# One PSUM bank, two kinds of turn: reads by VectorE in one quarter, writes by TensorE in the next

## The chip, the cores and the metric

The kernel runs on one core of one Trainium2 chip. The metric is the device time of the whole kernel in microseconds, here the median of three runs. The core has five engines with a queue of instructions each: TensorE (PE in the profile, its weight loads PEld), VectorE (DVE), ScalarE (ACT), GpSimd (POOL) and SyncE (SP), and 16 DMA engines. Each engine takes its instructions in the order in which they were written; semaphores make an instruction wait for one on another engine.

## The reference

The input is 16 images of 64 channels and 128 x 128 pixels, in f32. Four layers follow each other, each with a group normalisation ahead of it and a residual sum around it:

```python
x = x + L0(_gn(x))   # gram = xf xf^T / N;  y = gram xf;  out = conv_w y   (all 64 x 64 per image)
x = x + L1(_gn(x))   # |Scharr x| + |Scharr y| of each channel
x = x + L2(_gn(x))   # shift of some channels by a column, 3x3 convolution, bias
x = x + L3(_gn(x))   # 3x3 convolution, 1x1 convolution, batch norm over all images, leaky ReLU, clip
```

`_gn(v)` divides channels into 32 groups of two, subtracts the mean of a group in one image and divides by its standard deviation. So each image needs, between two layers, a few numbers per channel that come from sums over the image. The batch norm of the last layer needs sums over all images.

## The kernel before

Channels lie on 64 of the 128 partitions; the other 64 hold the other half of the image (or the other parity of its rows). An image is worked in eight chunks of eight rows (`NS` = 8, `R` = 8).

The main loop runs over steps (`step`), and each step over four quarters (`q` = 0 to 3). In one step, up to four stages work on different images: `Layer3` on image b from step 8b + 35, `Layer2` from 8b + 25, `Front` (layer 0 and the Scharr filter of layer 1) from 8b + 15, and `Gram`, which turns image rows into columns and builds the 64 x 64 product of an image that the front needs later. From image 7 on `Gram` takes eight steps for an image, for images 1 to 6 four. So the first some 20 steps are a ramp, in which stages come in one by one, and then eight steps repeat for each image. When all images are through, the last pass reads two arrays back, applies the batch norm and writes the output.

Nothing is scheduled: `InOrder` (line 63) keeps every engine's instructions in the order in which the Python code names them, and all of them show line 73 in the profile. Where an instruction stands in its engine's queue is thus set by step, quarter, and place within the quarter.

The small operations that turn sums into coefficients are written as generators, here called chains. After the work of a quarter, `tick()` (line 257) lets each live chain run to its next `yield`. There are two kinds.

- `coefficients` (line 280) makes the group norm's scale and shift from 16 partial sums: a reduction to `s2` on DVE, a product with a constant matrix on PE that averages over the group, then `rstd`, which computes a square root on ACT and one correction on DVE. It is started in quarter 0, by `Front` in step 8b + 23 and by `Layer2` in step 8b + 33.
- `gram_chain` (line 304) computes, from the Gram matrix of image b, the 128 x 128 weights `abd` of layer 0 and the coefficients of the next group norm. It has seven links of a product on PE and small DVE work on its result: with `gs` (to `gd`), `st`, `dd`, `rc`, `ad` (with `vv`), `pp`, and `st1`; after the second and the last product `rstd` follows with a root on ACT. For images 2 to 6 it starts at the end of a step, in quarter 3; from image 7 it starts in quarter 2 of step 8b - 9, and the `while` in it holds it until step 8b - 4.

All products of all chains go to one bank of PSUM, `bank` (lines 178 to 185): `sm(n)` hands out columns of it. From image 7 the Gram product itself also accumulates there. A read by DVE in the bank and a write by PE in it are ordered by semaphores even where they touch different columns, so a product waits for all reads that are written ahead of it, and a read for all products ahead of it.

Names that recur below: `one` and `two` are the PSUM tiles of a 3 x 3 convolution, `c` is the copy of `one` that ACT makes (lines 896 and 954), `d` the differences of rows that DVE makes for it, `qd` its shifted copies (by a DMA from POOL's queue in layer 2, by ACT in layer 3), `xh` the normalised rows for the Scharr filter, `u` and `e` its working tiles on DVE, of which ACT takes the absolute values, `xw` the columns for the Gram product, `sd` the result of a root, `nv` its operand, `junk` the output of a square whose sum is kept.

Of the kernel before, what the change touches and what calls it, by code (L numbers as in the profile page):

```python
# [21 lines left out]
NS = HH // R  # L22
EARLY = 3
# [85 lines left out]
def tile_kernel(ctx: ExitStack, tc: tile.TileContext, x, cw_h, w2_t, b2, wbin_t, w1_t, b1, gamma, beta, consts, out):  # L109
# [10 lines left out]
    def k(name):  # L120
        return kc[:, AT[name][0]:AT[name][1]]
# [41 lines left out]
    def sv(name, n=1):  # L163
        return small.tile([P, n], F32, tag=name, name=name)
# [6 lines left out]
    def small_product(dst, wt, src):  # L171

        for o in (1 - last[0], last[0]):
            pe.matmul(dst[cols(o)], wt[:, cols(o)], src, start=True, stop=True)
        last[0] = o
# [5 lines left out]
    def sm(n, rows=P):  # L181
        if n > 8:
            return bank[0:rows, P:P + n]
        turn[0] = (turn[0] + 1) % 16
        return bank[0:rows, 8 * turn[0]:8 * turn[0] + n]
# [67 lines left out]

    now = [0]
    chains = []

    def tick():
        for c in list(chains):
            if next(c, chains) is chains:
                chains.remove(c)  # L260

    def rstd(mE, r, me, eps=None):

        dve.tensor_copy(me, mE)
        nv = sv("nv")
        dve.scalar_tensor_tensor(nv, me[:, 0:1], me[:, 0:1], me[:, 1:2], op0=ALU.mult, op1=ALU.subtract)
        if eps is not None:
            dve.tensor_scalar_sub(nv, nv, eps)
        sd = sv("sd")
        act.activation(sd, nv, AF.Sqrt, scale=-1.0)  # L270
        yield
        r0 = sv("r0")
        dve.reciprocal(r0, sd)

        e = sv("e")
        dve.scalar_tensor_tensor(e, nv, r0, r0, op0=ALU.mult, op1=ALU.mult)
        dve.tensor_scalar(e, e, 0.5, 1.5, op0=ALU.mult, op1=ALU.add)
        dve.tensor_mul(r, r0, e)

    def coefficients(st, put, back=None):  # L280

        s2 = sv("s2", 2)
        dve.tensor_reduce(s2, st, axis=AX.X, op=ALU.add)
        yield
        pm = sm(2)
        small_product(pm, k("gmean"), s2)
        yield
        co = sv("co", 2) if back is None else sv("co2", 6)
        me = sv("me", 2)
        r, mean = co[:, 0:1], me[:, 0:1]  # L290
        yield from rstd(pm, r, me, GN_EPS)
        dve.scalar_tensor_tensor(co[:, 1:2], mean, -1.0, r, op0=ALU.mult, op1=ALU.mult)
        if back is not None:

            dve.reciprocal(co[:, 2:3], r)
            dve.tensor_mul(co[:, 3:4], co[:, 2:3], k("left"))
            dve.tensor_mul(co[:, 4:5], co[:, 2:3], k("right"))
            dve.tensor_add(co[:, 5:6], mean, back)
        put(co)
# [4 lines left out]
    def gram_chain(b, pg):  # L304

        gs = stp.tile([P, C + 1], F32, tag="gs", name=f"gs_{b}", bufs=2)
        if b > 2 * EARLY:
            dve.tensor_reduce(gs, pg.rearrange("p (j c) -> p c j", j=3), axis=AX.X, op=ALU.add)
        else:
            dve.tensor_copy(gs, pg)  # L310
        if b > 1:
            yield
        while b > 2 * EARLY and now[0] < NS * b - 4:
            yield
        gd = sm(C + 1)
        small_product(gd, k("same"), gs)
        yield
        g = stp.tile([P, C + 1], F32, tag="g", name=f"g_{b}", bufs=1)
        dve.tensor_scalar_mul(g, gd, 1.0 / HW)
        mu = g[:, C:C + 1]  # L320
        st = sv("st0", 2)
        dve.tensor_copy(st[:, 0:1], mu)

        junk0 = stp.tile([P, C], F32, tag="junk0", name=f"junk0_{b}", bufs=1)
        dve.scalar_tensor_tensor(
            junk0, g[:, 0:C], GN_EPS, k("Id"), op0=ALU.add, op1=ALU.mult, accum_out=st[:, 1:2]
        )
        if b > 1:
            yield
        pm = sm(2)  # L330
        small_product(pm, k("gavg"), st)
        yield
        r, me = sv("r"), sv("me", 2)
        yield from rstd(pm, r, me)

        vv = sv("vv", 3)
        dve.tensor_copy(vv[:, 0:1], mu)
        dve.tensor_sub(vv[:, 1:2], mu, me[:, 0:1])
        dve.tensor_scalar_mul(vv[:, 2:3], me[:, 0:1], -1.0)
        dd = stp.tile([P, 2, C], F32, tag="dd", name=f"dd_{b}", bufs=1)  # L340
        for s in range(2):
            dve.tensor_scalar_mul(dd[:, s, :], k("Id"), vv[:, s:s + 1])
        if b > 1:
            yield

        pr = sm(2 * C)
        small_product(pr, k("all"), dd.rearrange("p s c -> p (s c)"))
        yield

        t0 = stp.tile([P, C], F32, tag="t0", name=f"t0_{b}", bufs=1)  # L350
        dve.scalar_tensor_tensor(t0, pr[:, 0:C], vv[:, 0:1], g[:, 0:C], op0=ALU.mult, op1=ALU.subtract)
        cs = stp.tile([P, 2, C], F32, tag="cs", name=f"cs_{b}", bufs=1)
        for s in range(2):
            dve.scalar_tensor_tensor(cs[:, s, :], pr[:, C:2 * C], vv[:, 1:2], t0, op0=ALU.mult, op1=ALU.subtract)
        rc = stp.tile([P, C], F32, tag="rc", name=f"rc_{b}", bufs=1)
        dve.tensor_scalar(rc, cwh, r, 0.5, op0=ALU.mult, op1=ALU.mult)
        csf = cs.rearrange("p s c -> p (s c)")
        if b > 1:
            yield
        pq = sm(C)  # L360
        small_product(pq, csf, rc)
        yield
        r2 = sv("r2")
        dve.tensor_mul(r2, r, r)
        for s in range(2):
            rows = slice(s * C, (s + 1) * C)
            dve.tensor_scalar_mul(wbd[rows, rows], pq[rows], r2[rows])
        ad = stp.tile([P, C], F32, tag="ad", name=f"ad_{b}", bufs=1)
        dve.scalar_tensor_tensor(ad, pq, r2, k("Id"), op0=ALU.mult, op1=ALU.add)
        abd = stp.tile([P, P], F32, tag="abd", name=f"abd_{b}", bufs=EARLY + 3)  # L370
        dve.tensor_add(abd, wbd, k("I"))
        if b > 1:
            yield
        pd = sm(C + 3)
        small_product(pd[:, 0:C], csf, ad)
        small_product(pd[:, C:C + 2], abd, vv[:, 0:2])
        small_product(pd[:, C + 2:C + 3], wbd, vv[:, 2:3])
        yield
        pp = stp.tile([P, 2, C], F32, tag="pp", name=f"pp_{b}", bufs=1)
        dve.tensor_mul(  # L380
            pp, pd[:, 0:C].unsqueeze(1).to_broadcast([P, 2, C]), ad.unsqueeze(1).to_broadcast([P, 2, C])
        )
        av = sv("av", 3)
        dve.tensor_copy(av, pd[:, C:C + 3])
        if b > 1:
            yield
        pk = sm(1)
        small_product(pk, pp.rearrange("p s c -> p (s c)"), k("q"))
        if b > 1:
            yield  # L390
        bias = av[:, 2:3]
        st1 = sv("st1", 2)
        dve.tensor_add(st1[:, 0:1], av[:, 0:1], bias)
        t = sv("t1")
        dve.scalar_tensor_tensor(t, av[:, 1:2], av[:, 1:2], pk, op0=ALU.mult, op1=ALU.subtract)
        dve.scalar_tensor_tensor(
            st1[:, 1:2], st1[:, 0:1], st1[:, 0:1], t, op0=ALU.mult, op1=ALU.subtract
        )
        if b > 1:
            yield  # L400
        pm = sm(2)
        small_product(pm, k("gavg"), st1)
        yield

        co = stp.tile([P, 5], F32, tag="co1", name=f"co1_{b}", bufs=EARLY + 3)
        r, mean = co[:, 0:1], co[:, 3:4]
        yield from rstd(pm, r, co[:, 3:5], GN_EPS)
        dve.scalar_tensor_tensor(co[:, 1:2], bias, mean, r, op0=ALU.subtract, op1=ALU.mult)
        dve.reciprocal(co[:, 2:3], r)
        lead[b] = abd, co  # L410
# [18 lines left out]
    def first_gram():  # L429
# [30 lines left out]
        for link, _ in enumerate(gram_chain(0, pg)):  # L460
            if link in (2, 3, 4, 5, 6):
                rows_to_columns(1, link - 2, rows[link - 2])

    class Gram:
# [5 lines left out]
        def at(self, i, q):  # L470
            b = self.b
            n = 4 * (i - NS) + q

            self.part({1: 44, 5: 42, 9: 42}.get(n, 0))
            if n == 10:
                chains.append(gram_chain(b, self.pg))

            if i == 2 and q == 0:
                for m in range(3):
                    self.load(m)  # L480
            m = {11: 0, 13: 1, 15: 2, 19: 3, 21: 4, 23: 5, 27: 6, 31: 7}.get(4 * i + q)
            if m is not None:
                rows_to_columns(b, m, self.xr.pop(m))
                if m + 3 < NS:
                    self.load(m + 3)
# [603 lines left out]
    while chains:  # L1089
        tick()  # L1090
# [80 lines left out]
```

## Time and profile before

| | us |
|---|---|
| median of three runs | 2755.46 (2754.84 to 2756.58) |
| the profiled execution | 2756.86 |
| its span, first to last instruction | 2755.1 |
| PE busy | 2159.6 (78%) |
| DVE busy | 2192.4 (80%) |
| ACT busy | 2113.5 (77%) |
| POOL busy | 943.2 (34%) |
| mean granted TensorE clock | 0.896 |

Busy time is the sum of an engine's instructions, without waits. A share of the span is an average over stretches that have different limits, so the table alone doesn't say what bounds the kernel. Times in the views of the profile count from the start of the span. A wait is given as the engine and tile that waited, an arrow, and the engine and tile that ended last before the wait was over; a wait for several semaphores is put down to the last of them.

### The profile page before, as it was taken

What the parts mean: (1) busy time and instruction counts of PE and PEld (TensorE: products, weight loads), DVE (VectorE), ACT (ScalarE), POOL (GpSimd) and SP (SyncE); (2) the same over time, 40 slices, a digit from 0 to 9 for tenths busy, and PEclk for the clock granted to TensorE, in tenths of its full rate; (3) what the DMA queues carried; (4) which work ended last, traced back from release to release, by engine and by line L of the source; (5) the groups of instructions that cost most, each with busy time, mean ns of one, the idle gap of its engine ahead of it and who ended that gap; (6) DMA issues with size and microseconds to landing.
All of it is one profiled execution on the core that took longest, in us unless ns stands there. A gap on an engine that the chain in (4) does not pass through costs nothing. (4 is left out here: it accounts for less than half of the span.)

```text
span 2755.1 us, 46091 instructions
## 1 busy us (share of the span) xinstructions
PE 2159.6 (78%) x14804; PEld 886.9 (32%) x14804; DVE 2192.4 (80%) x3623; ACT 2113.5 (77%) x3177; POOL 943.2 (34%) x1350
## 2 busy tenths in 40 slices
PE   6578799999999999999999999999999994000000
PEld 4233333434343434343434343333334641000000
DVE  4998899899999999999999999999996335333332
ACT  4766779998989898989898989899997667333332
POOL 2055444444444444444434444454544300000000
PEclk8689899999999999999999999999999997555555
DMA  8799779898888898888888887888887768999999
GB/s 206 200 229 233 196 183 249 214 244 220 235 224 233 215 240 224 234 227 224 230 228 226 223 203 192 208 207 206 216 207 192 219 191 297 419 420 420 420 420 384
DMA packets 693601, 685.96 MB, mean 249 GB/s; under 512 B 60096, under 2 KB 580448, under 8 KB 693360
## 3 DMA queue, kind: packets, MB, share of 16 engines
q1 hardware_dynamic: 668208, 613.83, 76.0%
q0 software_dynamic: 25152, 69.18, 9.9%
q8 instruction: 119, 1.95, 0.3%
q14 instruction: 122, 1.00, 0.1%
HBM read 346.23 MB, written 268.44 MB: 223 GB/s over the span
## 5 line engine op out<-in xcount | busy, mean ns | idle before, releaser
L73 PE MATMUL two<-d,w 128*64 128x508 f32 (+2 forms) x2560 | 837.5, 587 | 0.0
L73 PE MATMUL two<-d,wi 128*64 128x508 f32 (+3 forms) x1536 | 572.7, 578 | 0.0
L73 POOL DMA_DIRECT2D qd<-d x512 | 270.8, 531 | 851.5 <-issue 295.8
L73 PE MATMUL two<-qd,pk 128*64 128x512 f32 (+1 forms) x1024 | 518.3, 587 | 10.1 <-DMA qd<-d 8.8
L73 POOL TENSOR_SCALAR edges<-v,co 64x8 f32<-64x8 f32 x512 | 397.7, 777 | 287.4 <-ACT v L73 204.0
L73 DVE TENSOR_TENSOR d<-v 128x512 f32<-128x512 f32 (+1 forms) x512 | 346.5, 679 | 58.4 <-issue 29.7
L73 PE MATMUL one<-v,w 128*64 128x508 f32 (+2 forms) x1600 | 364.6, 580 | 30.1 <-ACT c L73 30.1
L73 PEld LDWEIGHTS two<-d,w 128*64 128x64 f32 x2560 | 265.8, 136 | 326.3 <-issue 289.8
L73 PE MATMUL one<-v,wi 128*64 128x508 f32 (+3 forms) x1536 | 360.6, 602 | 1.5 <-issue 1.4
L73 ACT COPY qd<-d 64x512 f32<-64x512 f32 x512 | 315.5, 616 | 18.6 <-DVE d L73 12.5
L73 DVE SCALAR_TENSOR_TENSOR e<-e 128x1032 f32<-128x1032 f32 (+1 forms) x256 | 313.2, 1223 | 0.0
L73 ACT ACTIVATE xh<-po,co 128x128 f32<-128x128 f32 (+1 forms) x480 | 274.9, 621 | 31.0 <-PE po L73 24.9
L73 POOL TENSOR_SCALAR v<-v,kc 128x9 f32<-128x9 f32 x256 | 246.7, 976 | 11.9
L73 ACT ACTIVATE u<-u 128x1024 f32<-128x1024 f32 x128 | 135.7, 1060 | 144.2 <-DVE u L73 144.2
L73 PEld LDWEIGHTS two<-d,wi 128*64 128x64 f32 x1536 | 177.5, 136 | 193.5 <-issue 179.2
L73 ACT ACTIVATE v<-x,co 128x512 f32<-128x512 f32 (+2 forms) x368 | 235.0, 705 | 0.0
L73 DVE SCALAR_TENSOR_TENSOR y<-two,c 128x1024 f32<-128x1024 f32 x128 | 156.0, 1219 | 94.0 <-ACT v L73 68.2
L73 PE MATMUL po<-x,abd 64*64 64x512 f32 (+1 forms) x1024 | 177.7, 641 | 43.9 <-ACT xh L73 41.6
L73 PEld LDWEIGHTS one<-v,w 128*64 128x64 f32 x1600 | 124.6, 136 | 227.9 <-issue 139.5
L73 PEld LDWEIGHTS two<-qd,pk 128*64 128x64 f32 x1024 | 136.0, 136 | 151.1 <-issue 101.9
L73 DVE SCALAR_TENSOR_TENSOR u<-xh 128x1170 f32<-128x1170 f32 x128 | 175.4, 1371 | 4.8 <-ACT xh L73 4.5
L73 PEld LDWEIGHTS one<-v,wi 128*64 128x64 f32 x1536 | 109.3, 139 | 195.9 <-issue 188.3
(165 smaller groups left out, 3321.0 us busy)
## 6 DMA issues: line engine op xcount, KB each, us to landing
x<-in_x SPq DMA_DIRECT2D x256, 256.0 KB, 4.6
x_d<-u SPq DMA_DIRECT2D x512, 128.0 KB, 4.0
y_d<-y SPq DMA_DIRECT2D x512, 128.0 KB, 3.8
x_d<-x SPq DMA_DIRECT2D x496, 128.0 KB, 2.8
xr<-in_x SPq DMA_DIRECT2D x120, 512.0 KB, 6.5
qd<-d POOLq DMA_DIRECT2D x256, 130.0 KB, 3.1
qd<-d POOLq DMA_DIRECT2D x256, 129.8 KB, 3.9
v<-x_d SPq DMA_DIRECT2D x448, 72.1 KB, 2.9
```

Source lines behind the costliest of these rows:

```text
L73: return self.tc.keep_in_program_order(call(*args, **kwargs))
```

## The change

A counter `turn_of` is raised at the head of each tick, so it is odd in the ticks of quarters 0 and 2 and even in those of quarters 1 and 3. `when(TENSOR)` ahead of a product lets the chain wait until an even tick; `when(VECTOR)` stands ahead of the first read of a gram chain. All chains then read the bank in odd ticks and write it in even ones. In a gram chain from image 7 on, the `while` now stands ahead of the `yield`. Chains of images 0 and 1 keep their order but for the products in `coefficients`.

```diff
+    turn_of = [0]
+    VECTOR, TENSOR = 1, 0
+
+    def when(who):
+
+        while turn_of[0] % 2 != who:
+            yield
 
     def tick():
+        turn_of[0] += 1
         for c in list(chains):
             if next(c, chains) is chains:
                 chains.remove(c)
...
         dve.tensor_reduce(s2, st, axis=AX.X, op=ALU.add)
         yield
+        yield from when(TENSOR)
         pm = sm(2)
         small_product(pm, k("gmean"), s2)
...
         gs = stp.tile([P, C + 1], F32, tag="gs", name=f"gs_{b}", bufs=2)
+        if b > 1:
+            yield from when(VECTOR)
         if b > 2 * EARLY:
             dve.tensor_reduce(gs, pg.rearrange("p (j c) -> p c j", j=3), axis=AX.X, op=ALU.add)
         else:
             dve.tensor_copy(gs, pg)
+        while b > 2 * EARLY and now[0] < NS * b - 4:
+            yield
         if b > 1:
             yield
-        while b > 2 * EARLY and now[0] < NS * b - 4:
-            yield
+            yield from when(TENSOR)
         gd = sm(C + 1)
         small_product(gd, k("same"), gs)
...
         if b > 1:
             yield
+            yield from when(TENSOR)
         pm = sm(2)
         small_product(pm, k("gavg"), st)
```

The same line is added in the same way ahead of the other five products of `gram_chain` (`pr`, `pq`, `pd`, `pk` and the last `pm`).

More of the change, by code (lines that the diff above doesn't have):

```diff
@@ L344, in gram_chain @@
             yield
+            yield from when(TENSOR)
         pr = sm(2 * C)
@@ L359, in gram_chain @@
             yield
+            yield from when(TENSOR)
         pq = sm(C)
@@ L373, in gram_chain @@
             yield
+            yield from when(TENSOR)
         pd = sm(C + 3)
@@ L386, in gram_chain @@
             yield
+            yield from when(TENSOR)
         pk = sm(1)
@@ L400, in gram_chain @@
             yield
+            yield from when(TENSOR)
         pm = sm(2)
```

## The prediction

> **What bounds the kernel now.** I read first the busy time by stretch, to see who is full where. Columns: stretch, length, then busy us (and instructions) of PE, weight load, DVE, ACT, POOL, granted clock, DMA share, GB/s.
>
> ```profile
> 47.00:176.00 129.00, 75.63 (x990) 42.68 (x992) 122.74 (x202) 87.53 (x124) 19.48 (x22) 0.72 0.75 192
> 286.00:325.00 39.00, 25.09 (x121) 9.16 (x119) 31.17 (x70) 25.11 (x36) 16.85 (x20) 0.78 0.84 210
> 490.00:1690.00 1200.00, 1178.09 (x8304) 466.48 (x8302) 1143.40 (x1936) 1101.35 (x1721) 519.19 (x746) 1.00 0.86 225
> 2290.00:2755.00 465.00, 12.91 (x53) 4.73 (x52) 161.00 (x146) 167.25 (x147) 0.00 (x0) 0.52 1.00 405
> ```
>
> Until 176 us DVE is the bound (95% busy) and PE idles; between 286 and 325 nobody is full; from 325 on PE is 98% busy at full clock; the last 455 us are DMA at 100% and start when PE ends. So a microsecond gained or lost on PE after 325 us moves the end one for one. Second, whom PE waits for: between 286 and 318 us (first three lines), and from 345 to 2290 us (last two).
>
> ```profile
> PE bank L73 <- DVE g L73: 7.3, 1, 7.3
> PE bank L73 <- DVE dd L73: 4.2, 1, 4.2
> ...
> PE one L73 <- ACT c L73: 30.1, 27, 1.9
> ...
> PE bank L73 <- DVE rc L73: 0.4, 1, 0.4
> ```
>
> In the 1945 us of the steady part PE waits 0.7 us in all for the shared bank (rc 0.4, av 0.3): there is nothing for the change to win there. It can win in the ramp, where one pair of waits stands out. Third, the timeline there (start, length, operation, idle before it):
>
> ```profile
> 292.59 0.17 DVE L73 TENSOR_REDUCE s<-st 128x2 f32<-128x16 f32 x1 [0.67 <-ACT junk L73]
> ...
> 298.30 0.22 DVE L73 TENSOR_SCALAR g<-bank 128x65 f32<-128x65 f32 x1
> ...
> 298.57 0.38 PE L73 MATMUL bank<-s,kc 128*64 128x2 f32 x4 [7.34 <-DVE g L73]
> ...
> 306.34 0.16 DVE L73 COPY me<-bank 128x2 f32<-128x2 f32 x1 [6.28 <-PE bank L73]
> ```
>
> This is step 33. The product of s has its operand at 292.76, but another chain (image 5) reads the same bank in the same quarter, behind four Sobel operations, and PE is held until 298.5. Then image 5's product stands in PE's queue behind 7.4 us of Layer2, and DVE's read of the other result waits for that: 6.28 us. Fourth, the place in the steady part where PE waits for ACT, around steps 88 to 90:
>
> ```profile
> 1212.34 0.69 ACT L73 ACTIVATE c<-one,b_sb 128x512 f32<-128x512 f32 x1
> 1214.44 0.56 DVE L73 TENSOR_TENSOR d<-v 128x384 f32<-128x384 f32 x1
> 1215.95 1.19 ACT L73 COPY xw<-xr 128x1024 f32<-128x1024 f32 x1
> 1218.46 1.06 ACT L73 ACTIVATE u<-u 128x1024 f32<-128x1024 f32 x1 [1.32 <-DVE u L73]
> ...
> 1231.35 0.17 DVE L73 TENSOR_REDUCE s<-st 128x2 f32<-128x16 f32 x1 [1.73 <-ACT junk L73]
> ...
> 1240.66 0.20 ACT L73 ACTIVATE sd<-nv 128x1 f32<-128x1 f32 x1 [1.41 <-DVE nv L73]
> 1241.49 1.08 PE L73 MATMUL one<-v,w 128*64 128x512 f32 x4 [1.69 <-ACT c L73]
> ```
>
> From u at 1218.46 ACT runs without a wait to the square at 1230; that square holds DVE's s by 1.73, DVE then runs through to nv, nv holds ACT's root, the root holds c, and c holds PE 1.69 us. So lateness of ACT at 1218 reaches PE undiminished.
>
> [...] s's product waits for a read of other columns. [...] c stands behind the root that waits 1.41. [...] Here `one` took 5.34 us at 298.81 after the 7.34 us stall and 2.79 at 1249.49.
>
> **The change, part by part.** A tick runs once a quarter; odd turns are quarters 0 and 2 (DVE reads), even ones 1 and 3 (PE writes). A coefficients chain begins in quarter 0, so its product is already in quarter 1: nothing moves. A gram chain's first product moves from quarter 0 to 1; after its first root it waits one quarter more. So its first products go one quarter later, and everything after the first root two.
> *No instruction is added or removed on any engine, and no DMA is in these chains.* On PE a product is 0.2 to 0.5 us wherever it stands. Up to 176 us DVE is full and its work is the same: 0. PE's stalls there (5.94 us before an st product at 123 us) go or stay unseen, DVE covering them. In 176 to 286 PE's waits for dd and ad (3.4, 1.7, 2.0) shift; behind them DVE's d waits for POOL's v or for a twin DMA in most steps, so I count 0, and 2.2 as the upper end (0.9 at step 27 or 31, 1.3 at step 29).
> *Step 33:* image 5's g is read in quarter 2, so s's product needs only s and gs: DVE's `me` loses its 6.28 wait and PE reaches `one` at about 294 instead of 298.81 (wi is the next operand, written 292.68 to 293.8). On DVE: -6.3.
> *Step 34:* the product of dd moves from quarter 1 to 3, so PE loses 4.24 more, 9 in all; DVE only has -6.3. But in the next three steps DVE waited for PE 1.82, 1.79 and 3.37 (7.0 together, at 343, 355 and 364), so it can follow: -4.2. Sum of the ramp: **-10.5** (6.3 if the 4.2 is lost, 12.7 with the 2.2).
> *Steady, images 7 to 13:* the last root and its three DVE operations move from step 8b-1, quarter 2, to step 8b, quarter 0; the six after it (1.1 us) from 8b-1, quarter 3, to 8b, quarter 1. In step 88: DVE's d ended at 1215.00; it comes 1.1 earlier, then me, nv, nv take 0.55 to 0.6: nv is ready at 1214.5, root at 1214.6. ACT was free at 1212.34, so c and all behind it (normalisations, the xw copy) slip 2.27. Of this 1.31 is covered by ACT's wait before u; rest about **0.9**, and by the fourth view it reaches PE. I worked the same out for each image: 0.85 to 0.87 in all seven, since the steps repeat to 0.05 us. Images 14 and 15 have no xw copies left in ACT (wait before u 2.9 and 2.4): 0. Image 6: its six operations fall into step 41, quarter 1, ahead of the coefficients' nv: +1.04, less 0.55 for the root gone from step 40: +0.5. Sum: 7 x 0.86 + 0.5 = **+6.5** (0 if ACT finds the time elsewhere; 8 x 2.27 = 18 if the cover is missing).
> *Other steps of a chain:* the first root, into quarter 0 of step 85: nv at 1161.5, ACT free at 1161.5: +0.1, behind a 1.16 wait. abd into quarter 2 makes DVE 0.6 later at step 86, where its d waited 0.48 for PE: 0. The new products in quarter 3 need DVE results 3 to 5 us older: 0 (image 15, without gram parts, loses 1.0 on PE at step 118 before a 1.19 wait for ACT: 0).
> Net -10.5 + 6.5 = -4.0 on the profiled execution of 2756.86 (span 2755.1 and 1.8 around it): 2752.9. It lies 1.4 over the median of the runs, 2755.46: **2751.5**.
>
> **Rivals.** Faster: the ramp gain as above, and the roots cost nothing because ACT gets ahead elsewhere in the image: 2755.5 - 10.5 = 2745. For it: ACT is 92% busy, not full. Against: c of step 87 waits for PE's `one` (0.52), so nothing gained earlier survives it. Slower: the cover of 1.31 before u in quarter 2 is not there, because DVE's Sobel, now relieved by 1.1 us ahead of it, is no longer what ACT waits for, or the late c also holds PE's next `one` (1217.0, 2 us behind c): then 2.27 an image, 8 x 2.27 = 18, less 10.5: 2763. It decides for slower from 2.0 us an image (10.5 + 5.5 over 8). Third: PE's stall at step 33 only changes its name, for instance a half clock through 294 to 300 (2.5 us) or the twin DMA of step 34: ramp -4, steady +6.5, 2758. That the change does not do what it says is excluded: in the order of the changed program's instructions s's product precedes g's read.
>
> **Chances.** 0.2% is 5.5 us, about what a measurement of this kernel can tell from no change. Main case 0.45 (within); faster rival 0.30, and 0.05 for a ramp gain of 12 with half the loss; slower rival 0.15; third 0.05, split between within and slower, since its end lies near the 5.5. Faster 0.35, within 0.47, slower 0.18. The main case by itself spans 2748 to 2757; the range reaches the faster rival and most of the slower one: 2744 to 2762.
>
> **What would show it.** Right: no PE wait for g and no DVE wait for me near 290 us; PE reaching its full stretch some 10 us earlier; a new ACT wait for nv of about 2.2 us before c in steps 56, 64, ... 104; PE's wait of 1.5 to 1.8 for c two steps later grown to about 2.5, the sum of 30.1 to some 36. Wrong: those waits for c as before (gain 10), or above 3.5 (slower); or a new PE or DVE wait on the bank in the steady part, which I have at nil.

## The result and the profile after

The changed kernel takes 2749.73 us (median; 2747.79 to 2753.39) against 2755.57 us for the kernel before on the same chips: a ratio of 0.9981, 95% interval 0.9972 to 0.9990. It is 5.8 us faster, just past what this measurement can tell from no change. The prediction was 2751.5. Its profiled execution took 2749.49 us (span 2747.7), 7.4 us less than the profiled execution before.

The busy time by stretch of the changed kernel comes first (columns as before: stretch, length, busy us and instructions of PE, weight load, DVE, ACT, POOL, then granted clock, DMA share, GB/s).

```profile
47.00:176.00 129.00, 78.36 (x993) 44.98 (x994) 123.68 (x203) 87.65 (x124) 20.68 (x23) 0.71 0.76 195
286.00:325.00 39.00, 32.30 (x144) 11.59 (x146) 38.06 (x80) 33.34 (x49) 18.18 (x27) 0.87 0.95 251
490.00:1690.00 1200.00, 1177.28 (x8286) 471.27 (x8282) 1137.76 (x1936) 1093.20 (x1710) 465.14 (x745) 1.00 0.86 225
2290.00:2755.00 465.00, 5.78 (x22) 2.05 (x20) 158.54 (x142) 161.52 (x138) 0.00 (x0) 0.51 0.99 402
```

Only the second row has changed much in what fills the engines: between 286 and 325 us DVE is now busy for 38.06 of 39 us (31.17 before) and PE for 32.30 (25.09). What was a stretch in which nobody was full is one where DVE is. As the changed kernel is some 12 us ahead by then, part of this is the work of later steps. POOL's 54 us less in the third row lie on an engine that is far from full in both kernels; I have not followed them. In the last row PE's part has shrunk from 12.91 to 5.78 us, because PE ends earlier.

Whom PE waits for in the changed kernel, between 286 and 318 us (first two lines, the longest waits) and between 345 and 2290 us (last three):

```profile
PE two L73 <- DMA qd<-d: 4.4, 1, 4.4
PE bank L73 <- DVE gs L73: 2.7, 1, 2.7
...
PE one L73 <- ACT c L73: 34.1, 26, 2.6
PE two L73 <- DMA qd<-d: 1.9, 2, 1.5
PE bank L73 <- DVE ad L73: 1.1, 1, 1.1
```

The waits of 7.3 us for g and 4.2 us for dd are gone; DVE's 6.28 us wait for `me` is gone too. In their place stands one that was not there: 4.4 us for a twin transfer. In the steady part the sum of PE's waits for c has grown from 30.1 to 34.1 us, and that of its waits for twins has fallen from 6.3 to 1.9.

Step 33 on PE, and the new wait of step 34:

```profile
286.40 0.34 PE L73 MATMUL bank<-gs,kc 128*64 128x65 f32 x4 [2.68 <-DVE gs L73]
286.60 0.28 PE L73 MATMUL bank<-s,kc 128*64 128x2 f32 x4
287.17 4.38 PE L73 MATMUL one<-v,wi 128*64 128x512 f32 x12 [0.29 <-DVE wi L73]
...
309.49 1.09 PE L73 MATMUL two<-qd,pk 128*64 128x512 f32 x1 [4.43 <-DMA qd<-d]
```

The product of s follows that of gs at once, and `one` starts at 287.17, where it started at 298.81 before. Steps 88 and 90, ACT first and then PE:

```profile
1204.88 0.20 ACT L73 ACTIVATE sd<-nv 128x1 f32<-128x1 f32 x1 [2.06 <-DVE nv L73]
1204.99 0.67 ACT L73 ACTIVATE c<-one,b_sb 128x512 f32<-128x512 f32 x1
...
1208.60 1.17 ACT L73 COPY xw<-xr 128x1024 f32<-128x1024 f32 x1
1209.65 1.06 ACT L73 ACTIVATE u<-u 128x1024 f32<-128x1024 f32 x1
...
1232.49 4.46 PE L73 MATMUL one<-v,w 128*64 128x512 f32 x12 [2.17 <-ACT c L73]
```

Here the last root of an image's gram chain holds c, as forecast (the `one` that c copies had ended at 1202.22, and ACT starts c at 1204.99, behind the root); the 1.32 us wait before u is used up; and two steps later PE waits 2.17 us for c instead of 1.69. The `one` behind that wait took 4.46 us where it took 2.78 before, at a granted clock of 0.62 in this stretch.

To see where the time went I compare starts of the same product (`one`, in the step and quarter named) in the two traces. The table is worked out from the traces: start in that kernel less start in the kernel before, each counted from the start of its span, in us. It holds the experiments told below too. (Leads quoted in the expectations are counted from another zero, 0.2 us away for the changed kernel.)

```
step.quarter            26.2   33.2   36.0   45.0   56.0   88.0  112.0  144.0   PE's end
changed kernel          -5.1  -11.6  -12.5  -11.4  -11.4   -9.5   -7.6   -6.8   -7.1
images 2 to 6 only      -6.1  -14.6  -14.1  -13.4  -13.4  -13.6  -13.5  -13.3  -13.8
images 7 to 15 only     +0.4   +0.8   -1.6   -1.7   -1.6    0.0   +1.6   +1.9   +1.6
image 5 only            +0.3   -5.1   -4.9   -4.6   -4.6   -4.8   -4.8   -4.9   -5.1
images 2, 3, 4, 6       -5.5   -7.6   -8.0   -7.8   -7.8   -8.1   -8.1   -7.8   -8.2
image 3 only            -5.8   -3.5   -5.4   -5.5   -5.4   -5.0   -5.0   -4.8   -5.3
last root late only     +0.4   +2.9   +1.4   +1.4   +1.4   +3.8   +5.3   +6.0   +5.8
two quarters earlier    -6.2  -11.7  -13.7  -12.7  -12.6  -12.2  -11.8  -11.6  -12.1
four quarters earlier   -5.6  -11.8  -12.5  -11.6  -11.7  -13.3  -16.5  -17.3  -17.9
root after c            -4.2   -9.6   -8.8   -8.1   -8.0  -10.8  -12.2  -11.5  -12.0
operations late         -5.8  -12.9  -13.8  -13.2  -13.0  -17.1  -19.8  -19.7  -20.2
six quarters earlier    -6.0  -11.9  -14.1  -13.1  -12.1  -12.4  -12.4  -13.4  -13.9
ten quarters earlier    -6.1  -12.1  -14.2  -13.5  -11.1   -5.8   -1.8   -2.7   -3.1
```

The first row is the whole case: 12.5 us are won by step 36, and 5 are given back, about 0.6 an image. Two kernels whose ramp is that of before stand at -1.6 and +1.4 at step 36, so one trace tells the ramp to no better than about 1.6 us. The slope is far steadier: where the later images run as before, the lead changes by 0.4 us at most between steps 56 and 112. The first row also shows what the prediction did not have: over 7 of the 12 us (7.5 in step 32) were won before step 33 was reached.

### The profile page after: what moved, and what is told of

It is laid out like the page before. It is cut to its first block, busy times and chain, and to the rows that moved or that the text cites. A ratio compares the mean times of both kernels' runs of the same rounds, so it can differ in the third digit from the quotient of the medians.

```text
span 2747.7 us, 46085 instructions
## 1 busy us (share of the span) xinstructions
PE 2160.8 (79%) x14804; PEld 898.2 (33%) x14804; DVE 2190.5 (80%) x3623; ACT 2111.1 (77%) x3177; POOL 864.4 (31%) x1350
## 5 line engine op out<-in xcount | busy, mean ns | idle before, releaser
L73 POOL TENSOR_SCALAR edges<-v,co 64x8 f32<-64x8 f32 x512 | 341.9, 668 | 330.6 <-ACT v L73 222.5
L73 PE MATMUL one<-v,w 128*64 128x508 f32 (+2 forms) x1600 | 370.2, 587 | 34.1 <-ACT c L73 34.1
L73 PE MATMUL one<-v,wi 128*64 128x508 f32 (+3 forms) x1536 | 353.9, 592 | 1.4 <-issue 0.6
L73 ACT COPY qd<-d 64x512 f32<-64x512 f32 x512 | 315.6, 616 | 18.2 <-DVE d L73 12.2
L73 POOL TENSOR_SCALAR v<-v,kc 128x9 f32<-128x9 f32 x256 | 223.6, 886 | 11.9
L73 ACT ACTIVATE v<-v,co 128x1154 f32<-128x1154 f32 x128 | 172.0, 1344 | 7.3 <-DMA v<-x_d 7.2
```

What stands on the lines that cost most here:

```text
L73: return self.tc.keep_in_program_order(call(*args, **kwargs))
```

## The experiments

In those that choose images, `turn_to` in the gram chain takes the place of `when`: it waits as `when` does if the image is `gated`, and else not at all; images that are not gated run as before, with the order of their waits too. Where all chains take turns, the changed kernel is the base. Each time is a median with its ratio to the kernel before on the same chip.

**The two halves of the change, apart.**

```diff
+        gated = b in range(2, 2 * EARLY + 1)
...
-            yield from when(TENSOR)
+            yield from turn_to(TENSOR)
```

> The chains of images 2 to 6 take turns as in the changed kernel; those of images 7 to 15 run as before. Theory (the roots of the later images cost about 4.3 us, seen as the lead of PE falling from 11.2 at step 45 to 6.9 at step 122): the lead of about 11 us stays to the end, 2744.5 us against 2755.6 before. Rival (the lead is lost in the steady part whatever the chains do there): about 2749.7, as the changed kernel.

Measured: 2745.75 against 2756.35, 0.9958 (0.9945 to 0.9970). The lead of 13.4 us at step 56 is 13.8 at PE's end. The theory holds, the rival falls.

```diff
+        gated = b in range(2 * EARLY + 1, B)
```

> Only the chains of images 7 to 15 take turns. Theory: nothing is won before 345 us, and 4.3 us are lost from step 56 on: 2760 us. The recorded 0.86 an image would give 2761.5. Rival (the roots cost nothing, the loss came from elsewhere): 2755.6, as before.

Measured: 2758.77, 1.0010 (1.0002 to 1.0018), 2.4 us slower. In the trace the loss from step 56 to step 112 is 3.2 us, 0.46 an image. PE's waits for c in this kernel:

```profile
PE one L73 <- ACT c L73: 32.6, 27, 2.2
```

It is a loss of its own, so the rival (0) falls, narrowly by the runs (the interval begins at 0.6 us) and clearly by the trace; its size is about half of the 6 that the recorded 0.86 an image gives. The two halves add up to -8.2 by medians, the changed kernel has -5.8; the intervals allow the difference.

**Which chain wins in the ramp.** Step 33 is the only step in which the turns take apart a meeting of image 5's chain and Layer2's coefficients, and the prediction had put the whole gain there.

```diff
+        gated = b in (5,)
```

> Only image 5's chain, the one that meets Layer2's coefficients in step 33, takes turns. Recorded prediction (all of the ramp's gain is in steps 33 and 34): -10.5, so 2745 us. Reading of the changed kernel's trace (steps 33 and 34 add only 5 us to a lead of 7 that was there at step 32): 2750.5.

Measured: 2750.02 against 2756.35, 0.9974 (0.9963 to 0.9984), 6.3 us faster (4.4 to 10.2 by the interval). The recorded -10.5 falls, if narrowly, and the reading of the trace holds. PE led by 12.0 us at `one` of step 34 (304.78 against 316.80 us), so both halves of the predicted 10.5 did arrive there. Then it stood:

```profile
304.78 2.74 PE L73 MATMUL one<-v,wi 128*64 128x512 f32 x12
...
316.61 1.08 PE L73 MATMUL two<-qd,pk 128*64 128x512 f32 x1 [6.16 <-DMA qd<-d]
```

The product waits 6.16 us for the twin of a difference d that DVE finished at 309.3 us, 7.3 us earlier, and the lead falls to 4.9. Up to 6.1 of the 7.3 lie between issue and landing of the transfer. It was no slower than before: in the kernel before the two transfers of this place took 5.5 and 5.8 us, and landed 2.5 us ahead of PE. DVE's own lead was 5.7 to 6.0 us in steps 34 and 35; behind DVE and this transfer PE kept 4.9.

```diff
+        gated = b in (2, 3, 4, 6)
```

> The chains of images 2, 3, 4 and 6 take turns, image 5's does not, so the meeting in step 33 stays. Recorded prediction (0 for the steps up to 32, 0.5 lost at image 6): 2756. Reading of the changed kernel's trace (7 us won in steps 26 to 32, about 1 lost at step 42): 2749.5, if the stall of step 33 does not grow by what DVE has won before it.

Measured: 2750.28, 0.9976 (0.9966 to 0.9985), 6.1 us faster with the meeting of step 33 still there (PE waits 5.8 us for g in this kernel, 7.3 before). So the steps that the prediction had at 0 win as much as the one it built on. -6.3 and -6.1 make -12.4; both together gave -10.6.

```diff
+        gated = b in (3,)
```

> Only image 3's chain (steps 24 to 29) takes turns; PE's 3.39 us wait for dd at step 26 and its 1.72 for ad at step 27 belong to it. Recorded prediction (such waits are covered, since DVE's d waits for POOL's v or a twin DMA anyway): 0, so 2756. Reading of the traces with images 2, 3, 4 and 6 changed (DVE's lead grows from 2.0 to 5.0 us between steps 26 and 28): 3 us stay, 2753; the wait for dd gone, and the DVE waits for POOL's v fewer.

Measured: 2750.68 against 2755.48, 0.9983 (0.9975 to 0.9991), 4.8 us faster. In the trace PE leads by 3.5 at step 33 and by 1.9 more at step 36; the latter lie within what equal ramps differ by there. Of the 3.5, 1.1 stood in DVE's lead at 161 us already, before image 3's chain begins, so the trace shows 2.4. The runs (2.5 to 6.9 by the interval) leave room for the theory's 3 and none for the recorded 0. PE's waits for dd and ad are gone; waits of 2.2 us for rc and 3.7 for twins have come, and yet the gain stays. Why nothing covers these waits is seen in the kernel before, at step 27, where PE (first lines) and DVE (last line) read:

```profile
197.92 0.34 PE L73 MATMUL bank<-ad,cs 128*64 128x64 f32 x4 [1.72 <-DVE ad L73]
...
198.37 4.46 PE L73 MATMUL one<-v,wi 128*64 128x512 f32 x12
...
207.11 1.03 PE L73 MATMUL two<-d,wi 128*64 128x508 f32 x4
...
208.22 0.69 DVE L73 TENSOR_TENSOR d<-v 128x512 f32<-128x512 f32 x1 [2.84 <-issue]
```

DVE's wait of 2.84 us carries the name "issue", that is, nothing that the profile shows. But the last PE product that reads the old d ends at 207.11 + 1.03 = 208.14, and DVE overwrites d at 208.22. DVE waits for PE to be done with the buffer. PE is late there by its 3.39 us wait for dd in the step before, by its 1.72 us wait for ad, and by a `one` of 4.46 us (clock 0.60) behind it. POOL's v, done at 206.28, would have held DVE too, but for 0.9 us only. So most of DVE's wait was not a cover over PE's stall but its echo. In the kernel with image 3 alone changed:

```profile
205.05 0.69 DVE L73 TENSOR_TENSOR d<-v 128x512 f32<-128x512 f32 x1 [1.82 <-issue]
```

The same d starts 3.2 us earlier (1.1 of them from before the chain), 0.05 us after PE's last read of the old one ended at 205.00, and the wait is 1.0 us shorter. At step 31 of the kernel before the picture is the same: PE's last read ends at 270.37, and d starts at 270.44 after 2.50 us of "issue". That the releaser is PE's read is read from these times and from the code; no run took that one buffer away.

**What the steady loss is made of.**

```diff
+        for _ in range(2 if b > 2 * EARLY else 0):
+            yield
         pm = sm(2)
         small_product(pm, k("gavg"), st1)
```

This stands in the kernel before, ahead of the last product alone.

> The kernel before, with one thing moved: for images 7 to 15 the last product, the last root and what follows come two quarters later, so the root is in step 8b, quarter 0; all other steps, and images 2 to 6, stay. Theory (the last root alone makes the steady loss): as with turns for images 7 to 15 alone, 2.4 us over before, 2758.8 (2760.5 if the moved first root had been giving 0.2 an image back). Rival (the whole chain's order makes it): 2756.3, as before.

Measured: 2761.51 against 2756.06, 1.0019 (1.0012 to 1.0025), 5.5 us slower (3.3 to 6.9 by the interval), more than the 2.4 that was expected first. 3.9 of them come between steps 56 and 112, 0.56 an image. ACT's wait for nv in quarter 0 of step 8b is 2.05 to 2.06 us in each of the seven images, as in the changed kernel (2.05 to 2.07). Step 88:

```profile
1218.21 0.20 ACT L73 ACTIVATE sd<-nv 128x1 f32<-128x1 f32 x1 [2.06 <-DVE nv L73]
```

Moving the last root, together with the DVE operations ahead of it and behind it, makes the loss alone; the rest of the chain's reordering is not needed for it.

```diff
-        while b > 2 * EARLY and now[0] < NS * b - 4:
+        while b > 2 * EARLY and now[0] < NS * b - 5:
             yield
+        for _ in range(2 if b > 2 * EARLY else 0):
+            yield
```

> All chains take turns as in the changed kernel, but those of images 7 to 15 begin two quarters earlier, so that the last root and its operations are back in step 8b-1, quarters 2 and 3, while products and reads still alternate. Theory (what costs in the steady part is the place of the last root): the loss of 4 to 5 us is gone, about 2746, as with images 2 to 6 alone. Rival (it costs that products wait for the odd quarters): 2750, as the changed kernel.

Measured: 2744.77, 0.9959 (0.9947 to 0.9972). With the root back in quarter 2 of step 8b-1 the steady loss is gone (12.6 at step 56, 12.1 at the end), though products still wait for odd quarters. The rival falls.

```diff
-        act.activation(sd, nv, AF.Sqrt, scale=-1.0)
+        for _ in range(later):
+            yield
+        act.activation(sd, nv, AF.Sqrt, scale=-1.0)
```

(`later` is 1 for the last root of images 7 to 15, else 0.)

> The changed kernel, but for images 7 to 15 ACT's last root comes one quarter after DVE's nv, in step 8b, quarter 1, behind c, the normalisations and the xw copy; the six operations follow in quarter 2. Theory (the loss is ACT waiting for nv ahead of c): 0.2 us of root in place of a 2.15 us wait, so 2746 (up to 2748 if the six operations hold DVE's quarter 2). Rival (the loss is DVE's time in step 8b): 2750.

Measured: 2743.26, 0.9951 (0.9938 to 0.9963). The root's wait is gone in all seven images, and the loss with it; more than that, PE gains 0.6 us an image from step 56 to 112 (8.0 to 12.2). This I had not expected. The run moved two things, the root and, by a quarter, the six operations behind it, so it does not say which of them won the 0.6. Nor had I expected the next:

```diff
-        while b > 2 * EARLY and now[0] < NS * b - 4:
+        while b > 2 * EARLY and now[0] < NS * b - 5:
```

> As the run before, but four quarters earlier: the last root in step 8b-1, quarter 0, the first in 8b-4, quarter 0. Theory, if every quarter 0 has DVE's nv late because it stands behind Sobel and d there: ACT waits about 2 us for it as in step 8b, and 2750 comes out. If step 8b is a particular case (the first root in quarter 0 of step 8b-3 waits only 0.1 us): 2746.

Measured: 2738.91, 0.9937 (0.9925 to 0.9949), faster than either expectation. The waiting that the theory asked for is there, and costs nothing. ACT in step 87 of this kernel:

```profile
1182.44 0.20 ACT L73 ACTIVATE sd<-nv 128x1 f32<-128x1 f32 x1 [2.07 <-DVE nv L73]
1182.55 0.67 ACT L73 ACTIVATE c<-one,b_sb 128x512 f32<-128x512 f32 x1
...
1186.15 1.05 ACT L73 ACTIVATE u<-u 128x1024 f32<-128x1024 f32 x1
...
1191.65 0.20 ACT L73 ACTIVATE sd<-nv 128x1 f32<-128x1 f32 x1 [1.45 <-DVE nv L73]
```

In step 87 of the kernel before ACT waits 1.30 before u, 0.37 and 0.31 before two roots and 0.52 before c: 2.50 us. 0.37 of them are the moved root's own; the other 2.13 are still more than its 2.07. Here u runs without a wait, and ACT is so far from late that it still waits 1.45 for the next root. Step 88 has only the 1.31 us before u. So in these two places the root's price is its wait less what ACT idles later in the same step. That explains why nothing is lost, not why 0.7 an image is won. For that the six DVE operations behind the root remain, which no longer stand in quarter 3 of step 8b-1, ahead of DVE's part of step 8b. They can be moved alone, with the root left in quarter 2 of step 8b-1:

```diff
         act.activation(sd, nv, AF.Sqrt, scale=-1.0)
         yield
+        for _ in range(later):
+            yield
```

(on the kernel that begins two quarters earlier; `later` is 4 for the last root of images 7 to 15)

> As the kernel whose chains of images 7 to 15 begin two quarters earlier (last root in step 8b-1, quarter 2, 2744.8), but the six DVE operations behind the last root come four quarters later, in step 8b, quarter 3, where DVE has 1.7 us of slack ahead of s. Theory (1.1 us of DVE ahead of the Sobel operation u of step 8b is what the wait for c at 8b+2 is made of): ACT's 1.30 us wait before u in step 8b falls to 0.2, PE gains 0.7 an image, 2740. Rival (the place of the root matters, not DVE's time): 2745.

Measured: 2737.60 against 2755.89, 0.9932 (0.9919 to 0.9944), the lowest median of all, though its interval overlaps that of four quarters earlier. In steps 88 and 90, ACT and PE with two quarters earlier, and then with the operations late:

```profile
1206.21 1.06 ACT L73 ACTIVATE u<-u 128x1024 f32<-128x1024 f32 x1 [1.31 <-DVE u L73]
...
1229.25 2.78 PE L73 MATMUL one<-v,w 128*64 128x512 f32 x12 [1.76 <-ACT c L73]
```

```profile
1200.36 1.06 ACT L73 ACTIVATE u<-u 128x1024 f32<-128x1024 f32 x1 [0.27 <-DVE u L73]
...
1223.39 2.78 PE L73 MATMUL one<-v,w 128*64 128x512 f32 x12 [0.73 <-ACT c L73]
```

The wait before u falls by 1.04 us, as expected from 1.1 us of operations; PE's wait for c two steps later falls from 1.76 to 0.73; and PE gains 6.8 us between steps 56 and 112, 0.96 an image. The theory holds, and so does its number for the wait; PE's gain is larger than the 0.7 an image that it gave. It also gives the changed kernel's loss and these gains one cause: PE's wait at step 8b+2 is set by when ACT's u of step 8b starts, and that is the later of ACT coming free (made late by the root in quarter 0) and DVE's u (made late by the six operations). The traces bear it out. Take the shift of u in step 8b against the kernel before, counted from the square that ACT does ahead of c, and beside it the shift of PE's `one` two steps later: in the changed kernel +0.8 and +0.6 us, with the root after c -0.5 and -0.5, with the operations late -1.0 and -1.0, with four quarters earlier -1.2 and -1.2, in all seven images but for one with the root after c (-0.2).

**Moving the chain further.**

```diff
-        while b > 2 * EARLY and now[0] < NS * b - 4:
+        while b > 2 * EARLY and now[0] < NS * b - 6:
             yield
+        for _ in range(2 if b > 2 * EARLY else 0):
+            yield
```

> All chains take turns; those of images 7 to 15 have the last root in step 8b-2, quarter 2, and the first in 8b-5, quarter 2. Theory (what PE sees two steps after 8b is DVE's time in steps 8b-1 and 8b, where the root's nine DVE operations stand): with them gone from there PE gains some 0.75 us an image as with four quarters earlier, 2739; less, if step 8b-2 has no room for them. Rival (four quarters earlier won for its root's place alone): 2745, as with two earlier.

Measured: 2743.63, 0.9957 (0.9944 to 0.9969). The theory's 2739 misses; the rival's 2745 is inside the interval, though its reason has fallen with the run just told.

With `NS * b - 7` in that line:

> As six earlier, but another four quarters: last root in step 8b-3, quarter 2, first in 8b-6, quarter 2. Theory: steps 8b-1 and 8b are as free of the chain's end as with six earlier, so the same 2739 within 3 us; 2745 if the chain's parts cost as much in their new steps.

Measured: 2754.29, 0.9997 (0.9989 to 1.0006). Both of its numbers miss. PE's waits from 345 to 2290 us, six quarters earlier and then ten:

```profile
PE one L73 <- ACT c L73: 18.6, 22, 2.8
PE two L73 <- DMA qd<-d: 10.3, 11, 2.0
PE bank L73 <- DVE rc L73: 5.0, 8, 0.7
```

```profile
PE one L73 <- ACT c L73: 26.7, 37, 1.9
PE two L73 <- DMA qd<-d: 5.6, 6, 2.6
PE bank L73 <- DVE rc L73: 5.0, 8, 0.6
PE bank L73 <- DVE av L73: 3.4, 9, 0.4
```

Steps 8b-1 and 8b are free in both, and in the first the waits for c are indeed 11.6 us fewer than with two quarters earlier (30.2). But the middle of the chain meets other steps: waits for rc and av, 0.4 and 0.3 with two quarters earlier, and more for the twins (10.3 in the first). Step by step, over images 8 to 13, what the theory asked for did come: from step 8b+1 to 8b+2 PE wins 1.2 us an image with six quarters earlier and 1.0 with ten. But between the starts of steps 8b-6 and 8b-3, where the middle of the chain now stands, it loses 1.3 with six and 3.1 with ten. The waits named account for only a part of this; the rest I leave open.

## Why the prediction was right, and where it was not

**The time** was right: 2751.5 against 2749.73, 1.8 us off. In part that was luck: two of its steps were wrong by about 6 us each, in opposite directions, and the sum hid it.

**"In 176 to 286 ... I count 0, and 2.2 as the upper end"**: this step failed. Some 7 us are won by step 32, and images 2, 3, 4 and 6 alone make the kernel 6.1 us faster (4.1 to 9.4 by the interval). The working had named the right waits (dd 3.4, ad 1.7 and 2.0) and set DVE's waits for POOL's v and for a twin against them, as if those stood there for another reason. For the two longest, 2.84 us at step 27 and 2.50 at step 31, that is wrong: they end with PE's last read of d. The working had put waits of the same name at 343 and 364 us down to PE, and these two not. Together they were 5.3 us between 176 and 286 us; in the changed kernel 1.9 are left there. DVE's waits for POOL's v fell too, from 3.9 to 1.6, but that they follow PE is not shown: at step 26 of the kernel before, POOL's v comes behind DVE's own d, a twin's issue and 6.0 us of `edges`. The working also left out the clock: `one` behind the waits of steps 26 and 27 took 5.3 and 4.46 us in the kernel before, at a granted clock of 0.50 and 0.60, and 2.74 and 2.79 in the changed one, at 1.00.

**Steps 33 and 34, -10.5**: mis-sized. The mechanism was right to the quarter: no wait for g, no wait for `me`, and PE 12.0 us ahead at step 34 with image 5 alone. Of its two terms -6.3 measured -5.7 to -6.0 on DVE (steps 34 and 35) and -4.9 on PE (step 36). The -4.2, which supposed that DVE would follow, is not there: a twin transfer took it, 6.2 us of wait with image 5 alone, 4.4 in the changed kernel. The third rival had named that transfer, as something that would take the ramp's gain down to 4; its mechanism came, and the gain of the other images outweighed it.

**Steady, +6.5**: right in place and cause, too large. ACT waits 2.05 to 2.07 us for nv in every image, c slips 2.27, u slips 0.82 (predicted 0.86). "By the fourth view it reaches PE" held for most of it: PE's `one` two steps later slips 0.6, and its wait for c grows by 0.15 to 0.65 us, 0.4 on average. Where the other 0.2 of u's slip go I have not traced. To this comes the clock: in two of the seven images `one` ran some 1.6 us longer behind the wait (4.39 and 4.46 us against 2.78, at a granted clock of 0.63 and 0.62), of which the wait for c of the next step (1.05 and 0.98 before, then gone) took back 1.0. In sum 0.56 an image. Images 14 and 15 and image 6, set at 0 and +0.5, cost about 0.8 and 1.0 in this trace.

**Rivals.** "The roots cost nothing" (2745) is what comes out when the root is put elsewhere, not of this change. The slower one (2.27 an image) did not come: the cover before u held.

**What would show it**: the waits for g and `me` gone, the new wait for nv, and PE's full stretch about 11 us earlier all came. The sum of waits for c grew to 34.1 rather than 36. One sign of being wrong came too, in small: new waits for the bank in the steady part, set at nil, sum to 1.7 us against 0.7 before. The largest, 1.1 us for ad at step 118, had been seen coming as a loss of 1.0 ahead of a wait for ACT.

## What to carry to other kernels

A waiting engine covers another's stall only if it waits for something that does not itself come from the stalled engine; ask of every wait that you set against a gain what it would do if the stall were gone, "issue" waits included, since DVE's 2.84 and 2.50 us for a buffer that PE still read had no other name in the views. A small operation that one engine makes another wait for had no price of its own here: in the two places measured it cost its wait less the idle time left in the same step behind it, nothing of 2.07 us in step 8b-1 and 0.8 of 2.06 us in step 8b. And when a move costs something, look at what else moved with it: the six DVE operations of 1.1 us together were worth 0.96 us an image, 6.8 over seven images, about as much as the whole change to the turns (5.8).

## What was not expected of the hardware

The prediction had a lower clock in its third rival alone, in the ramp at 294 to 300 us, and none in the steady part. In the kernel before there was none there: behind PE's seven waits for c of 1.69 to 1.91 us between 345 and 2290 us `one` took 2.78 us each time, at a granted clock of 1.00. In the changed kernel `one` took 4.48, 4.39 and 4.46 us at 436.57, 833.25 and 1232.49 us, behind waits for c of 2.56, 2.17 and 2.17 us, at a granted clock of 0.62 to 0.63. The length of the wait alone does not decide it: the five other images of 7 to 13 waited 1.93 to 2.17 us in the same kernel, and `one` took 2.78, again at 1.00. What does decide it the traces do not show.
